# A GNN stack: the last of four column blocks is transposed on VectorE and sent through DRAM

## The chip, the cores and the metric

The kernel runs on one core of a Trainium2 chip. The metric is the device time in microseconds (us). Three runs of the kernel before took 2336.9, 2339.27 and 2341.34 us; the median, 2339.27 us, is the time before. Engines are called PE (TensorE, the matmuls), DVE (VectorE), ACT (ScalarE), POOL (GpSimd) and SP (SyncE, which issues DMAs).

## The reference, cut to what matters

Four layers of a graph network act on `x` of 32 batches, 512 nodes and 64 features; each adds its result to `x`, after a layer norm and a ReLU. The change touches the last layer, two graph attention steps with shared adjacency `graph` (512 x 512):

```python
def gat_layer(x, graph, W, b):
    h = x @ W
    s = jnp.einsum('bnd,bmd->bnm', h, h) * graph
    s = jnp.where(s == 0.0, NEG_INF, s)
    a = jax.nn.softmax(s, axis=2)
    return jnp.einsum('bnm,bmd->bnd', a, h) + b
heads = jax.vmap(lambda W, b: gat_layer(flow_x, graph, W, b))(Wh, bh)   # 8 heads of 128
x = jax.nn.leaky_relu(cat, negative_slope=0.01)                          # cat: the heads side by side
out = gat_layer(x, graph, W_out, b_out)                                  # 64 features
return jax.nn.leaky_relu(out, negative_slope=0.01)
```

So for each batch and head a matrix of 512 x 512 scores is made, exponentiated, and multiplied with the features. All arithmetic is float32.

## The kernel before, in words

**Stages.** Up to about 470 us of the profile the kernel runs layers 0 to 2. From there on it runs the last layer, and only that stage is changed (the features `hn`, `hs` of the first two batches are made a little earlier).

**Units.** The stage works on 144 units, each two attention problems at once (k = 0, 1): 128 units of class `Heads` (two heads of one batch, four units a batch) and 16 of class `Out` (the last step of two batches). The 512 nodes are C = 4 blocks of P = 128. A unit passes through these steps, with r a row block and j a column block of its score matrices:

- `scores(r)` (L386): matmuls into the PSUM tile `s_ps`, of which there are two buffers.
- `soft(r, mid)`: two reductions on DVE (L372) read `s_ps`, add the mask and give `s_att` and the row extremes `negmax`; two exponentials on ACT (L365) write row block r of `p_att` and the row sums. `mid` is called between, on DVE behind the reductions: it is `normalize` of an earlier unit.
- `transpose(j)` (L399): PE turns column block j of `p_att` in 16 transposes of 64 x 64 into two PSUM tiles `pt_ps` (tag "m", three buffers, shared with `y_ps`, `g_ps`, `gT_ps` and others). ACT copies the first (L405), at once; DVE copies the second (L407), at the end of the slot. Together they are `pt_att`.
- `values(j)` (L414): two matmuls with `pt_att` are added into `av`.
- `recips` (L424 to L434): DVE takes the reciprocals of the row sums and turns them in blocks of 32 x 32 (L426); SP writes them in four pieces to DRAM (`rec_row`), and reads them back in two, spread over the partitions (`recb`).
- `normalize` (L443): DVE multiplies `av` by `recb`. For `Heads`, `row_halves` then multiplies by the head's weights (`y_ps`, L526), ACT adds the bias (`cat`, L534) and DVE does the leaky ReLU (L311).

**Slots.** `planned` interleaves the units. In slot k, unit u does the step whose offset is off = k - 4u: scores at -1 to 2, soft at 0 to 3, transposes at TR = 5 to 8, values at VA = 6 to 9, normalize at END = 9, recips at 5. So a unit starts every four slots, each slot holds the steps of three or four units, and "slot 0 to 3 of a unit" below means the offset modulo 4. Inside a slot the order on each engine is that of the calls in `slot`, and it is kept as written for PE, DVE and ACT; DMAs on SP and POOL are placed by the framework. On PE it is scores, then `row_halves`, transposes, values, products for `Out` (`gT_ps`, L565); where `row_halves` has work (`led`), transposes come after the values. On DVE it is the two reductions, `normalize`, the copy of `pt_ps`, the leaky ReLU, recips, and `prep_late`.

**Features.** Once a batch, in slot 2, `prep_late` of `Heads` normalizes the features (`hn`, L474 and L475), takes their greatest values for a check of special cases at the end (`least`, L478), and POOL multiplies them by the root of the degrees, twice, into both halves of `hs` (L483). PE transposes `hs` in slot 3 (`hx_ps`, L290), ACT copies it (`hx`, L292), and `g_ps` (L508) is made of it in the next slot.

Of the kernel before, what the change touches and what calls it, by code (L numbers as in the profile page):

```python
# [8 lines left out]
F32 = mybir.dt.float32  # L9
# [5 lines left out]
P = 128  # L15
# [7 lines left out]
def fast_form(  # L23
# [29 lines left out]
    G = min(8, B)  # L53
    NG = B // G
    F2 = 2 * F

    const = ctx.enter_context(tc.tile_pool(name="const", bufs=1))
    xpool = ctx.enter_context(tc.tile_pool(name="xpool", bufs=1))
# [254 lines left out]
    class Pair:  # L313
# [4 lines left out]

        def begin(self):
            self.p = pbuf.tile([P, 2, C, N], F32, name="p_att")
            self.sum = tiny.tile([P, 2, C], F32, name="sum_att")
            self.negmax = tiny.tile([P, 2, C], F32, name="negmax")
            self.pts = {}
# [55 lines left out]
        def scores(self, r):  # L381
# [3 lines left out]
            for k in range(2):  # L385
# [2 lines left out]
                    start=True, stop=True,  # L388
                )

        def transpose(self, j):
            pt = pbuf.tile([P, 2, N], F32, name="pt_att", bufs=2)
            self.pts[j] = [pt[:, k] for k in range(2)]

            ps = [ps_m.tile([P, 2, C, F], F32, name="pt_ps", tag="m") for half in range(2)]
            for k in range(2):
                for r in range(C):
                    for half in range(2):
                        nc.tensor.transpose(  # L399
                            ps[half][:, k, r],  # L400
                            self.p[halves(half), k, r, j * P : (j + 1) * P],
                            ident[halves(half), halves(half)],
                        )
            pth = pt.rearrange("p k (r half q) -> p k r half q", r=C, half=2)
            nc.scalar.copy(pth[:, :, :, 0, :], ps[0])  # L405

            return lambda: nc.vector.tensor_copy(pth[:, :, :, 1, :], ps[1])  # L407

        def values(self, j):
            pt = self.pts.pop(j)  # L410
            if j == 0:
                self.av = ps_v.tile([P, N], F32, name="av")
            for k in range(2):
                nc.tensor.matmul(  # L414
                    self.av[halves(k), :], lhsT=self.v(k, j), rhs=pt[k],
                    start=(j == 0), stop=(j == C - 1),
                )

        def recips(self):

# [36 lines left out]
    class Heads(Pair):  # L457
# [11 lines left out]
        def prep_late(self, step):  # L469
            b = self.b  # L470
            if step == -2 and self.i == 0:
                mean, rstd = (t[:, b % 2, :, None].to_broadcast([P, C, F]) for t in flow_stats[b // 2])
                h = early.tile([P, C, F], F32, name="hn3", bufs=3)
                nc.vector.tensor_tensor(h, xs[b // G][:, b % G], mean, OP.subtract)  # L474
                nc.vector.scalar_tensor_tensor(  # L475
                    h, h, 0.0, rstd, op0=OP.max, op1=OP.mult
                )
                nc.vector.tensor_reduce(  # L478
                    least[:, b * C : (b + 1) * C], h, AX.X, OP.max
                )  # L480
                hs = early.tile([P, C, 2, F], F32, name="hs3", bufs=2)
                for k in range(2):
                    nc.gpsimd.tensor_tensor(  # L483
                        hs[:, :, k, :], h, root_d[:, :, None].to_broadcast([P, C, F]), OP.mult
                    )
                Heads.hs[b] = hs
                Heads.hn[b] = h

# [160 lines left out]
    def planned(units, products):  # L649
# [15 lines left out]
        def slot(k):  # L665
            for u, r in at(k, -1):
                u.scores(r)

            led = list(led_in(k))
            for u, off in led:
                u.row_halves(off)

            while exps:
                exps.pop(0)()

            copies = []

            def transposes():  # L680
                for u, j in at(k, TR):
                    copies.append(u.transpose(j))

            if not led:
                transposes()
            for u, j in at(k, VA):
                u.values(j)
            for u, j in at(k, VA - 1, 1):
                u.make_v()
            for n, u in products:  # L690
                u.product(k - n * C)
            for u, j in at(k, -3 * C, 3 * C):
                u.prep_pe(j - 2 * C)
            if led:
                transposes()
            for u, j in at(k, END, 5):
                u.end_pe(j)

            def mid():
                for u, j in at(k, END, 1):  # L700
                    u.normalize()

            now = list(at(k, 0))
            for u, r in now:
                exps.append(u.soft(r, mid))
            if not list(led_in(k + 1)):
                while exps:
                    exps.pop(0)()
            if not now:
                mid()  # L710
            for copy in copies:
                copy()
            for u, j in at(k, END, 5):
                u.end_late(j)
            for u, j in at(k, TR, 1):
                u.recips()
            for u, j in at(k, -3 * C, 3 * C):
                u.prep_late(j - 2 * C)

# [971 lines left out]
```

## Time and profile before

| | |
|---|---|
| median of three runs | 2339.27 us |
| the profiled execution, its time | 2340.76 us |
| its span | 2338.9 us |
| PE busy | 2248.0 us, 19066 instructions |
| DVE busy | 1794.3 us, 4366 instructions |
| ACT busy | 1576.3 us, 3674 instructions |
| POOL busy | 68.4 us, 104 instructions |
| transposes L399 | 9216, 415.6 us busy |
| copies of `pt_ps`: DVE L407, ACT L405 | 576 of 687 ns, 576 of 582 ns |
| HBM read, written | 43.98 MB, 4.78 MB |

Busy times say how long an engine had an instruction in work; spans of neighbouring instructions overlap, so the time from start to start is what one really costs in a row. The chain that ended last goes back from the last instruction, at each step to what released it; its shares say where the time of the run lay. A row of the timeline begins with the start and the length in us; "x4" means that four instructions are merged in it. In a table by windows each row has a stretch, its length, then busy time and count of PE, PEld, DVE, ACT and POOL, the granted clock, the busy share of the DMA engines, and GB/s. On SP and POOL a DMA's row is the time to issue it; the transfer follows.

### The profile page before, as it was taken

The page shows a single profiled execution, that of the slowest core. Times are in us where ns is not written, and L with a number is a line of the kernel's source. Part 1 is how long each engine was busy: PE and PEld are TensorE (multiplying, and loading weights), DVE is VectorE, ACT ScalarE, POOL GpSimd, SP SyncE. Part 2 cuts the span into 40 slices and gives each one's busy share as a digit, 9 for nine tenths or more (in the row PEclk, how much of TensorE's full clock was granted, in tenths as well). Part 3 has the DMA queues.
Part 4 walks back from the last instruction along what each step waited for, and adds up shares of the span by engine and source line. Part 5 has one row for each costly group of instructions (what it writes and reads, how often), then busy time and mean ns, then how long its engine had stood idle before and what let it go on. Part 6 is the DMA issues. An engine that isn't in the chain of part 4 may idle for free.

```text
span 2338.9 us, 49561 instructions
## 1 busy us (share of the span) xinstructions
PE 2248.0 (96%) x19066; PEld 1086.8 (46%) x19066; DVE 1794.3 (77%) x4366; ACT 1576.3 (67%) x3674; POOL 68.4 (3%) x104
## 2 busy tenths in 40 slices
PE   7999998799999999999999999999999999999997
PEld 4676776644444444444444444444444444444443
DVE  6788878677878787878787878787878787878776
ACT  3444433287777777777777777677777777877775
POOL 2000000000000000000000000000000000000000
PEclk9999999599999999999999999999999999999999
DMA  4000000000001000000000000000000000000001
GB/s 125 1 1 1 2 1 1 1 24 20 29 20 29 20 29 19 29 20 29 20 28 20 29 20 29 19 29 20 29 20 28 20 29 20 24 20 24 24 20 39
DMA packets 44645, 53.11 MB, mean 23 GB/s; under 512 B 15928, under 2 KB 25312, under 8 KB 44272
## 3 DMA queue, kind: packets, MB, share of 16 engines
q1 hardware_dynamic: 43888, 49.65, 6.9%
q8 instruction: 152, 2.49, 0.5%
q14 instruction: 93, 0.76, 0.1%
q0 software_dynamic: 512, 0.20, 0.1%
HBM read 43.98 MB, written 4.78 MB: 21 GB/s over the span
## 4 chain that ended last, share of the span: by engine, by line
PE 72%; DVE 4%; POOL 2%; issue 1%; ACT 0%; DMA 0%; SPq 0%; POOLq 0%; DVEq 0%
PE s_ps L386 23%; PE av L414 23%; PE pt_ps L399 13%; PE y_ps L526 5%; PE gT_ps L565 5%; PE g_ps L508 2%; DVE pt_att L407 2%; POOL hs L483 2%; PE hx_ps L290 1%; DVE hn L475 1%; DVE s_att L372 1%; DVE hn L474 0%; DVE gs L583 0%; PE gV_ps L576 0%; PE back_ps L449 0%
## 5 line engine op out<-in xcount | busy, mean ns | idle before, releaser
L365 ACT ACTIVATE p_att<-s_att,negmax 128x512 f32<-128x512 f32 x1152 | 827.7, 723 | 0.0
L372 DVE CUSTOM_DVE_ANT_0 s_att<-s_ps,flow_neg 128x512 f32<-128x512 f32 x1152 | 739.5, 679 | 2.4 <-PE s_ps L386 2.1
L407 DVE COPY pt_att<-pt_ps 128x512 f32<-128x512 f32 x576 | 395.5, 687 | 281.2 <-PE pt_ps L399 226.6
L386 PE MATMUL s_ps<-hx,g 64*128 64x512 f32 x2048 | 570.0, 634 | 5.7 <-DVE negmax L372 5.1
L414 PE MATMUL av<-pt_att,hn 128*64 128x512 f32 x2048 | 552.3, 618 | 0.0
L399 PEld LDWEIGHTS pt_ps<-ident,p_att 64*128 64x128 f32 x9216 | 373.6, 138 | 375.0 <-issue 228.0
L405 ACT COPY pt_att<-pt_ps 128x512 f32<-128x512 f32 x576 | 335.3, 582 | 157.9 <-PE pt_ps L399 152.2
L399 PE MATMUL pt_ps<-ident,p_att 64*128 64x64 f32 x9216 | 415.6, 226 | 2.8 <-DVE pt_att L407 0.9
L534 ACT ACTIVATE cat<-y_ps,bh 128x512 f32<-128x512 f32 x256 | 162.2, 684 | 168.4 <-PE y_ps L526 168.4
L386 PEld LDWEIGHTS s_ps<-hx,g 64*128 64x128 f32 x2048 | 156.1, 187 | 243.6 <-DVE negmax L372 180.6
L365 ACT ACTIVATION_READ_ACCUMULATOR p_att<-s_att,negmax 128x1 f32 x1152 | 224.6, 195 | 0.0
L443 DVE TENSOR_TENSOR o_att<-av,recb 128x512 f32<-128x512 f32 x144 | 99.6, 692 | 140.5 <-PE av L414 139.1
L414 PEld LDWEIGHTS av<-pt_att,hn 128*64 128x64 f32 x2048 | 101.2, 134 | 156.8 <-PE s_ps L386 87.2
L311 DVE SCALAR_TENSOR_TENSOR cat<-cat 128x1024 f32<-128x1024 f32 x128 | 155.5, 1215 | 0.0
L924 PE MATMUL acc<-v,s 64*128 64x65 f32 x2048 | 132.5, 291 | 1.5 <-DVE rec L935 0.8
L924 PEld LDWEIGHTS acc<-v,s 64*128 64x128 f32 x2048 | 129.5, 206 | 6.9 <-issue 2.6
L565 PE MATMUL gT_ps<-cat,wo_sb 128*64 128x512 f32 x512 | 131.7, 593 | 0.0
L526 PE MATMUL y_ps<-o_att,wh_sb 64*128 64x512 f32 x512 | 131.6, 591 | 0.0
L520 ACT COPY g<-g_ps 128x512 f32<-128x512 f32 x128 | 68.8, 589 | 84.2 <-PE g_ps L508 84.2
L833 PE MATMUL nt_ps<-adj_t,hn 128*128 128x512 f32 x256 | 116.2, 597 | 0.8 <-DVE hn L797 0.8
L386 PE MATMUL s_ps<-gs 64*128 64x512 f32 x256 | 72.4, 642 | 24.2 <-DVE gs L583 24.2
L372 DVE DVE_READ_ACCUMULATOR2_ANT negmax<- 128x1 f32 x1152 | 95.3, 83 | 0.0
(166 smaller groups left out, 1571.7 us busy)
## 6 DMA issues: line engine op xcount, KB each, us to landing
recb<-rec_row SPq DMA_DIRECT2D x288, 128.0 KB
rec_row<-rect SPq DMA_DIRECT2D x576, 1.0 KB
out_dram<-y SPq DMA_DIRECT2D x32, 128.0 KB
x<-in_x_dram SPq DMA_DIRECT2D x3, 1024.0 KB
x<-in_x_dram SPq DMA_DIRECT2D x4, 256.0 KB
adj_raw<-in_adj_dram SPq DMA_DIRECT2D x1, 1024.0 KB
mask<-mask SPq DMA_DIRECT2D x4, 256.0 KB
wh_sb<-in_L_gnn_Wh_dram SPq DMA_DIRECT2D x2, 256.0 KB
```

What stands on the lines that cost most here:

```text
L311: nc.vector.scalar_tensor_tensor(t, t, 0.01, t, op0=OP.mult, op1=OP.max)
L365: nc.scalar.activation(self.p[:, k, r, :], ns[:, k], AF.Exp, bias=self.negmax[:, k, r : r + 1], scale=-1.0, accum_out=self.sum[:, k, r : r ...
L372: nc.vector.tensor_tensor_reduce(out=ns[:, k], in0=ps[:, k], in1=flow_neg[:, r], scale=-1.0, scalar=BIG, op0=OP.add, op1=OP.min, accum_out ...
L386: nc.tensor.matmul(ps[:, k], lhsT=g[halves(k), r * P : (r + 1) * P], rhs=x[halves(k), :], start=True, stop=True,)
L399: nc.tensor.transpose(ps[half][:, k, r], self.p[halves(half), k, r, j * P : (j + 1) * P], ident[halves(half), halves(half)],)
L405: nc.scalar.copy(pth[:, :, :, 0, :], ps[0])
L407: return lambda: nc.vector.tensor_copy(pth[:, :, :, 1, :], ps[1])
L414: nc.tensor.matmul(self.av[halves(k), :], lhsT=self.v(k, j), rhs=pt[k], start=(j == 0), stop=(j == C - 1),)
L526: nc.tensor.matmul(ps, lhsT=wh_sb[halves(k), h, :], rhs=self.o[halves(k), :], start=True, stop=True,)
L534: nc.scalar.activation(self.cat[:, k], pss[k], AF.Identity, bias=bh[:, h : h + 1], scale=1.0)
L565: nc.tensor.matmul(self.gps[halves(k), :], lhsT=wo_sb[:, h, :], rhs=Heads.cat[b + k, h], start=(h == 0), stop=(h == H - 1),)
L924: nc.tensor.matmul(self.acc[k][:, r], lhsT=self.s[b // 2][halves(k), b % 2, r * P : (r + 1) * P], rhs=self.v[halves(k), b], start=(b == 0) ...
```

## The change

1. Column block j = 3 is no longer transposed on PE. `transposes` runs for j = 0 to 2. A new step `turn(r)`, at offsets 2 to 5 and on DVE behind `normalize`, turns row block r of that column block in squares of 32 x 32, from `p_att` into the SBUF tile `turn` (128 x 256 elements each). After r = 1 and r = 3, POOL issues a write of two row blocks to DRAM (`turn_row`, 256 KB in pieces of 512 bytes).
2. `route`, called with `recips`, reads the squares back in transposed order into `turned`: four reads of 128 KB, 32 partitions each, in pieces of 1 KB; two are issued by POOL and two by SP. `values(3)` takes `turned` in two halves of 256 columns, in steps of 32 elements.
3. The second PSUM copy of j = 0 and j = 2 goes from DVE to ACT, right behind the first; that of j = 1 stays on DVE.
4. `hs` is made by one DVE operation of 128 x 512 ahead of the `least` reduction, in place of two POOL operations of 128 x 256 behind it.

In the changed program's order SP has, for each unit, the four `rec_row` writes, the first read of `turned`, the two reads of `recb`, and the second read of `turned`; POOL has two `turn_row` writes and then two reads of `turned`.

```diff
+        def turn(self, r):
+            if r == 0:
+                self.turns = wk.tile([P, Q, C // 2, 2, 2, 32], F32, name="turn")
+                self.rows = dram.tile([P, Q, C // 2, P], F32, name="turn_row")
+            nc.vector.transpose(
+                self.turns[:, :, r // 2, :, r % 2].rearrange("p a k i -> p k a i"),
+                self.p[:, :, r, N - P :].rearrange("p k (a i) -> p k a i", i=32),
+            )
+            if r % 2:
+                nc.gpsimd.dma_start(
+                    self.rows[:, :, r // 2],
+                    self.turns[:, :, r // 2].rearrange("p a k r i -> p a (k r i)"),
+                )
+
+        def route(self):
+            rows = self.rows.rearrange("(b i) a g x -> a i b (g x)", b=Q)
+            pt = wk.tile([P, Q, C // 2, 2, 2, 32], F32, name="turned")
+            for a in range(Q):
+                (nc.sync if a % 2 else nc.gpsimd).dma_start(
+                    pt[a * 32 : (a + 1) * 32].rearrange("p b g k r i -> p b (g k r i)"), rows[a]
+                )
+            self.pts[C - 1] = [
+                pt[:, :, :, k].rearrange("p b g r i -> p g r b i") for k in range(2)
+            ]
...
             nc.scalar.copy(pth[:, :, :, 0, :], ps[0])
+            if j != 1:
+                nc.scalar.copy(pth[:, :, :, 1, :], ps[1])
+                return None
...
             for k in range(2):
-                nc.tensor.matmul(
-                    self.av[halves(k), :], lhsT=self.v(k, j), rhs=pt[k],
-                    start=(j == 0), stop=(j == C - 1),
-                )
+                parts = 2 if j == C - 1 and len(pt[k].shape) > 2 else 1
+                for g in range(parts):
+                    n = N // parts
+                    nc.tensor.matmul(
+                        self.av[halves(k), g * n : (g + 1) * n], lhsT=self.v(k, j),
+                        rhs=pt[k][:, g] if parts > 1 else pt[k],
+                        start=(j == 0), stop=(j == C - 1 and g == parts - 1),
+                    )
...
+                hs = early.tile([P, C, 2, F], F32, name="hs3", bufs=2)
+                nc.vector.tensor_tensor(
+                    hs, h[:, :, None].to_broadcast([P, C, 2, F]),
+                    root_d[:, :, None, None].to_broadcast([P, C, 2, F]), OP.mult,
+                )
                 nc.vector.tensor_reduce(
                     least[:, b * C : (b + 1) * C], h, AX.X, OP.max
                 )
-                hs = early.tile([P, C, 2, F], F32, name="hs3", bufs=2)
-                for k in range(2):
-                    nc.gpsimd.tensor_tensor(
-                        hs[:, :, k, :], h, root_d[:, :, None].to_broadcast([P, C, F]), OP.mult
-                    )
...
-                for u, j in at(k, TR):
+                for u, j in at(k, TR, C - 1):
                     copies.append(u.transpose(j))
...
             if not now:
                 mid()
+            for u, r in at(k, 2):
+                u.turn(r)
             for copy in copies:
-                copy()
+                if copy:
+                    copy()
             for u, j in at(k, END, 5):
                 u.end_late(j)
             for u, j in at(k, TR, 1):
                 u.recips()
+                u.route()
```

Here Q = P // 32 = 4.

More of the change, by code (lines that the diff above doesn't have):

```diff
@@ L55, in fast_form @@
     F2 = 2 * F
+    Q = P // 32
     const = ctx.enter_context(tc.tile_pool(name="const", bufs=1))
```

## The prediction

> **What bounds the kernel now.** I read the busy times first, then the chain that ended last, then the timeline of one ordinary stretch, then the waits at the places that the diff touches. The long second stage (from about 470 us) is the one concerned.
>
> ```profile
> PE 2248.0 (96%) x19066; PEld 1086.8 (46%) x19066; DVE 1794.3 (77%) x4366; ACT 1576.3 (67%) x3674; POOL 68.4 (3%) x104
> PE 72%; DVE 4%; POOL 2%; issue 1%; ACT 0%; DMA 0%; SPq 0%; POOLq 0%; DVEq 0%
> PE s_ps L386 23%; PE av L414 23%; PE pt_ps L399 13%; PE y_ps L526 5%; PE gT_ps L565 5%; PE g_ps L508 2%; DVE pt_att L407 2%; POOL hs L483 2%; PE hx_ps L290 1%; DVE hn L475 1%; DVE s_att L372 1%; DVE hn L474 0%; DVE gs L583 0%; PE gV_ps L576 0%; PE back_ps L449 0%
> ...
> 600.00:1000.00 400.00, 390.75 (x3312) 168.84 (x3312) 309.11 (x784) 301.91 (x723) 8.30 (x14) 1.00 0.08 25
> ```
>
> The last row is 400 us of that stage: PE busy 390.75 of 400, DVE 309, ACT 302. PE is nearly solid and carries 72% of the chain; transposes (L399) alone are 13% of it. One slot on PE without extras:
>
> ```profile
> 1224.92 1.13 PE L386 MATMUL s_ps<-hx,g 64*128 64x512 f32 x4
> 1225.88 0.66 PE L399 MATMUL pt_ps<-ident,p_att 64*128 64x64 f32 x16
> 1226.47 1.08 PE L414 MATMUL av<-pt_att,hn 128*64 128x512 f32 x4
> 1227.48 1.13 PE L386 MATMUL s_ps<-hx,g 64*128 64x512 f32 x4
> ...
> 1226.70 0.69 DVE L372 CUSTOM_DVE_ANT_0 s_att<-s_ps,flow_neg 128x512 f32<-128x512 f32 x1
> 1227.32 0.69 DVE L407 COPY pt_att<-pt_ps 128x512 f32<-128x512 f32 x1
> ```
>
> Scores, 16 transposes, values, next scores: 2.56 us from start to start. In the chain these three are 1.06, 0.49 and 1.01 us. The scores at 1227.48 overwrite the s_ps that the reduction starting at 1226.70 frees at about 1227.32 (the copy's start), so DVE is only 0.16 us ahead of PE here. Unit periods, from the starts of the reciprocals (L424), repeat over nine units: 11.3, 13.3, 11.3, 14.9, 14.7, 13.7, 13.3, 11.9, 12.2 us, 116.5 in all.
>
> The place of the features:
>
> ```profile
> 1235.34 0.42 DVE L478 TENSOR_REDUCE least<-hn 128x4 f32<-128x256 f32 x1
> 1235.48 1.19 POOL L483 TENSOR_TENSOR hs<-hn,root_d 128x256 f32<-128x256 f32 x2 [47.43 <-DVE hn L475]
> 1235.20 1.08 PE L414 MATMUL av<-pt_att,hn 128*64 128x512 f32 x4
> 1236.72 0.66 PE L290 MATMUL hx_ps<-ident,hs 128*128 128x128 f32 x4 [0.44 <-POOL hs L483]
> 1237.31 1.13 PE L386 MATMUL s_ps<-hx,g 64*128 64x512 f32 x4
> ```
>
> PE ends its values at 1236.21 and waits 0.5 us for POOL's product, 32 times in the run.
>
> The two round trips through DRAM at the very end, and what a GpSimd transfer shows in the opening:
>
> ```profile
> 2323.52 1.16 DMA rec_row<-rect
> 2325.49 3.22 DMA recb<-rec_row
> ...
> 1224.00:1224.50 0.50, 0.50 (x4) 0.10 (x4) 0.50 (x3) 0.50 (x2) 0.00 (x0) 1.00 0.37 135
> 4.46 1.54 POOL L93 DMA_DIRECT2D wl<-in_L_gnn_net_params_dram  x3
> wg<-in_L_gnn_W_dram POOLq DMA_DIRECT2D x2, 16.0 KB, 4.8
> ```
>
> A small write lands 1.16 us after its issue; the second 128 KB read 3.22 us after. In an ordinary unit the reads issued from 1222.86 move data from about 1224.0 to 1225.9 (the DMA share, last but one figure of the row, is zero before), so 1.15 us pass before the first byte, and 1 us or so after the last.
>
> [...] The trace has only a 128x32 one, 0.21 us (L426), beside 0.19 for a 128x8 reciprocal[...]. [...] the trace has only the opening's 4.6 to 8.0 us beside bulk loads. [...] here recb waits for rec_row 278 times, 129.7 us.
>
> **The change part by part.** Column block 3's transposes go from PE: 144 units x 16, 0.49 us a group on the chain (0.65 only where the following scores shrink to 0.91, so the pair costs the same): 144 x 0.49 = -70.6 us, if PE stays the bound.
>
> Values of block 3 become four matmuls of 256 columns for two of 512. [...] The shape in steps of 32 columns isn't in the trace; 0.15 us at most, which is what this line already takes above the same-shaped gT_ps (1.01 against 0.86 us). I take 0.05: +7 us, ends +2 and +22.
>
> PSUM copies: DVE loses three of four (0.60 us from start to start), ACT gains two and loses one. ACT has per unit 8 exponentials at 0.71, five copies at 0.48, and cat: under 10 us of 11, and its copies come before the slot's exponentials, sooner than DVE's did. Cost 0, hidden by ACT's 100 us of slack in 400.
>
> DVE turns: four a unit, each 128x256. The nearest row, a 128x256 operation at L474, is 0.41 long; independent operations here follow 0.08 us before the end, so 0.37 apart. Bounds: 0.3, and 0.6 if it costs like a 128x512 copy. DVE per unit: -3 x 0.60 + 4 x 0.37 = -0.3 us. But where they stand counts. Slot 3 and 0 of a unit hold: two reductions 1.22, turn(1) 0.37, leaky 1.17, two reductions 1.22. Counted from the copy's end at 1223.14 this frees s_ps at 1227.12; PE, without block 3's transposes, asks at 1226.99. Stall 0.13 us in the three ordinary units of nine: 48 x 0.13 = +6 us. Where slot 0 also holds g_ps or gT_ps (0.86 us), PE arrives later and nothing is lost. turn(0) stands in the 0.8 us for which DVE waited for transposes anyway, turn(2) and turn(3) behind reductions.
>
> Features on DVE: one 128x512 product, 0.61 between starts, in place of two on POOL (1.19). They are ready at about 1236.0, so PE's 0.5 us wait goes. Nobody waits for least before the end. But it and both reductions of slot 3 now follow 0.61 later: these end at 1237.6, and the scores that began at 1237.31 wait for s_ps until 1237.65. g_ps then covers the rest; by slot 1 PE is 0.22 us ahead of before, not 0.49. So 32 x 0.27 = +8.6 us; ends -17 (the wait gone, no new one) and +15.
>
> The trip through DRAM. turn(3) stands behind normalize on DVE (0.61), itself behind the previous unit's last values; it ends 0.98 us after normalize starts. The values that need it start 1.1 us before the next normalize. So a unit can't be shorter than L + 2.1 us, L being the trip. Step by step: handoff to POOL 0.17 (1235.31 to 1235.48); its descriptors 1.0 (64 rows took 0.51; 512 rows aren't in the trace: 0.5 to 2.5); then 1.16 as for rec_row and 1.2 for 256 KB in 512-byte rows (the final outputs moved 256 KB in about 1 us). The write has landed at 3.5. On SP's queue the changed program stands so: four rec_row, the first turned read, two recb, the second turned read. All behind the first turned read wait for the write: four issues of 0.48, data of four transfers in a row on one queue from 1.15 to about 3.8, 1.0 to land: 4.8. POOL's two reads (0.6 us each to issue) are in before. L = 8.3, between 7 and 10.5: floor 10.4. The shortest unit would be 10.9, so nothing is lost. Queued behind them on SP stand only the next rec_row and, after an Out unit, the y writes, some 8 us later. turn(0) also waits for the writes of two units before, long landed. recb, held 2 us longer, lands by 8 us, and normalize needs it 1 us after the turned block: free, and late with it if L grows. In the drain the last unit (9.7 us) shows the floor: +2 us.
>
> Sum: -70.6 + 7 + 6 + 8.6 + 2 = -47 us. On the profiled execution (2340.76 us, 2338.9 of it span; the median, 2339.27, is 1.5 below): 2292 for the median.
>
> **The rivals.** (1) The trip is late; this one ends slower. Shortened units are 10.9, 12.9, 10.9, 14.4, 14.2, 13.2, 12.9, 11.4, 11.7, sixteen cycles of them. A floor of 12.0 costs 2.2 + 0.6 + 0.3 = 3.1 a cycle, 50 us: the gain is gone at L = 9.9. At L = 10.5 it is 5.5 x 16 = 88 us, 2380. For it: [...] an unmeasured size, two hops, and 4.6 us as the shortest GpSimd landing, of which two make 9.2. Against: that opening moved 232 to 376 GB/s, this stage 25. At L = 9.5 the loss is 26 us: 2318. (2) DVE becomes the bound: a turn of 0.69. Then 0.32 more in 48 + 32 places, +25 us: 2317. For: slack of 0.16[...]. (3) All of PE's time is won and the wait for features too: -70.6 - 17 = 2252. For: DVE falls by 0.3 a unit; against: the two places worked out above.
>
> **How the numbers follow.** Forecast 45%, own range 2275 to 2308; (3) 12%; (2) or a trip slightly late, 2308 to 2334, 16%; within 0.2% (4.7 us, about what a measurement can tell) 4%; (1) 23%. Faster 0.73, same 0.04, slower 0.23. The range, 2260 to 2368, leaves out about 5% below, and above it a trip over 10.3 us, 14%.
>
> **What would show it.** Right: L399 at 6912, its chain share near 10%; PE still over 95% in the stage; the values of block 3 hardly waiting for DMA; periods near 10.9 in the short units; scores after hx waiting for negmax. Wrong: PE waiting for turned in the short units, all nine periods levelled at one floor; POOL issues of over 2 us; turns of 0.6 us; or values on turned over 1.1 us.

## The result, and the profile after

The changed kernel takes 2350.9 us (median of five runs, 2348.07 to 2362.17) against 2339.06 us for the kernel before (five runs, 2336.09 to 2341.34). The ratio is 1.0059, with a 95% interval of 1.0033 to 1.0086: slower by 11.8 us, where 47 us less was forecast. The profiled execution's span is 2348.9 us, 10.0 more than before.

First the page of the changed kernel: busy times, and the chain that ended last, by engine and by line.

```profile
PE 2176.4 (93%) x17338; PEld 1037.8 (44%) x17338; DVE 1741.1 (74%) x4542; ACT 1635.4 (70%) x3818; POOL 400.2 (17%) x616
PE 49%; DMA 13%; DVE 8%; issue 7%; SPq 3%; POOL 1%; ACT 1%; DVEq 0%; POOLq 0%; ACTq 0%
PE av L449 16%; PE s_ps L389 16%; DMA turned<-turn_row 10%; PE pt_ps L427 6%; PE gT_ps L601 5%; PE y_ps L562 4%; SPq L470 3%; DVE s_att L375 3%; DMA turn_row<-turn 3%; DVE pt_att L438 2%; PE g_ps L544 2%; DVE hs L515 1%; DVE hn L511 1%; POOL turn_row L403 1%; DVE hn L510 0%
```

PE lost 71.6 us of work, but it also fell from 96% busy to 93%. The chain tells more: PE carries 49% of it where it carried 72%, and DMA, which had none, now carries 13%, of which the reads of `turned` are 10%. SPq, time in which SP was issuing, is new too, with 3% on L470, the reads of `recb`. The stretch of 400 us answers to the one shown of before:

```profile
600.00:1000.00 400.00, 376.34 (x2927) 159.49 (x2924) 296.82 (x819) 313.40 (x753) 79.67 (x124) 1.00 0.39 106
```

PE is busy for 376 us, not 391: 24 us of 400 idle, in a stage that left 9 idle before. What PE waited for, from the list of waits of the changed kernel (engine, line, releaser; us in total, times, longest):

```profile
PE av L449 <- DMA turned<-turn_row: 70.4, 64, 4.8
DVE o_att L479 <- PE av L449: 335.4, 144, 7.0
PE s_ps L389 <- DVE negmax L375: 22.4, 34, 0.7
```

Values of column block 3 waited for `turned` 64 times, 70.4 us in all. DVE's idle time ahead of `normalize` grew to 335 us. The third row is the place of the features. The same two places in the kernel before, which has no `turned`:

```profile
DVE o_att L443 <- PE av L414: 139.1, 143, 2.5
PE s_ps L386 <- DVE negmax L372: 5.1, 14, 0.4
```

From the timeline of the changed kernel, first a short slot with the leaky ReLU, and then the place of the features:

```profile
1246.27 1.18 DVE L312 SCALAR_TENSOR_TENSOR cat<-cat 128x1024 f32<-128x1024 f32 x1
1246.54 1.13 PE L389 MATMUL s_ps<-hx,g 64*128 64x512 f32 x4
...
1247.60 1.08 PE L449 MATMUL av<-pt_att,hn 128*64 128x512 f32 x4
...
1247.99 0.69 DVE L375 CUSTOM_DVE_ANT_0 s_att<-s_ps,flow_neg 128x512 f32<-128x512 f32 x1
...
1248.74 1.13 PE L389 MATMUL s_ps<-hx,g 64*128 64x512 f32 x4
```

```profile
1232.56 0.69 DVE L515 TENSOR_TENSOR hs<-hn,root_d 128x512 f32<-128x512 f32 x1
...
1233.17 0.41 DVE L519 TENSOR_REDUCE least<-hn 128x4 f32<-128x256 f32 x1
1233.50 0.66 PE L291 MATMUL hx_ps<-ident,hs 128*128 128x128 f32 x4
...
1234.11 0.68 DVE L375 CUSTOM_DVE_ANT_0 s_att<-s_ps,flow_neg 128x512 f32<-128x512 f32 x1
...
1234.86 1.13 PE L389 MATMUL s_ps<-hx,g 64*128 64x512 f32 x4 [0.71 <-DVE negmax L375]
```

Scores, values and next scores take 2.20 us from 1246.54 to 1248.74. Scores take 1.06 and values 1.01 in the chain, so 0.13 us is a stall: the last reduction starts only at 1247.99, behind the leaky ReLU. At the second place PE no longer waits for the features (`hx_ps` has no releaser), but the scores behind it wait 0.71 us for the reductions.

One trip through DRAM that came late, from the timeline of the changed kernel:

```profile
1240.49 0.69 DVE L479 TENSOR_TENSOR o_att<-av,recb 128x512 f32<-128x512 f32 x1 [1.44 <-PE av L449]
1241.10 0.43 DVE L398 STREAM_TRANSPOSE turn<-p_att 128x256 f32<-128x256 f32 x1
...
1241.83 0.71 POOL L403 DMA_DIRECT2D turn_row<-turn  x1 [5.65 <-DVE rec L460]
1241.89 1.29 SPq L465 DMA_DIRECT2D rec_row<-rect  x4
...
1244.64 0.32 SPq L412 DMA_DIRECT2D turned<-turn_row  x1
...
1245.13 1.42 SPq L470 DMA_DIRECT2D recb<-rec_row  x2
1245.15 1.14 POOL L412 DMA_DIRECT2D turned<-turn_row  x2 [2.61 <-PE s_ps L389]
...
1246.60 0.59 SPq L412 DMA_DIRECT2D turned<-turn_row  x1
1246.64 0.72 POOL L403 DMA_DIRECT2D turn_row<-turn  x1 [0.36 <-DVE turn L398]
...
1250.79 1.09 PE L449 MATMUL av<-turned,hn 128*64 128x256 f32 x8 [0.44 <-DMA turned<-turn_row]
```

turn(3) ends at 1241.53, POOL issues the write at 1241.83, and SP's first read, which waits for that write, starts at 1244.64, so by 3.11 us the write has landed. SP then issues two reads of `recb`, and only at 1246.60 the last read of `turned`. The values start at 1250.79, 9.26 us after the turn. The chain of the same stretch shows what released them:

```profile
1245.13 0.78 SPq L470
1245.96 0.59 SPq L470
1246.60 3.95 DMA turned<-turn_row
1250.79 1.09 PE av L449 x8
```

It runs through SP's two issues of `recb` into the last read of `turned`, which takes 3.95 us to land. And how much the DMA engines moved meanwhile, from a table by windows of the changed kernel:

```profile
1245.30:1246.40 1.10, 1.10 (x13) 0.36 (x9) 1.10 (x6) 1.10 (x5) 0.98 (x2) 1.00 0.52 118
1246.40:1248.00 1.60, 1.60 (x8) 0.50 (x8) 1.60 (x4) 1.60 (x5) 0.72 (x1) 1.00 0.69 204
1248.00:1250.40 2.40, 2.30 (x24) 0.96 (x20) 2.24 (x9) 2.04 (x7) 0.00 (x0) 1.00 0.92 247
1250.40:1252.00 1.60, 1.21 (x10) 0.78 (x12) 0.08 (x1) 1.60 (x4) 0.00 (x0) 1.00 0.00 0
```

After 1248.0 the engines are 92% busy at 247 GB/s until the block has landed, then at rest. From 1245.3 to then they moved some 1050 KB (118 GB/s for 1.1 us, 204 for 1.6, 247 for 2.4). The unit's four reads of `turned` (512 KB), its two of `recb` (256 KB) and a `turn_row` write of the next unit (256 KB, issued at 1246.64) make 1024.

Over the 63 units of the steady part whose values waited, the medians from the end of turn(3) are: write issued 0.30, SP's first read begins 3.12 (landed, as SP sees it), POOL's reads begin 3.62, the issue of SP's last read done 5.74, values 10.06 us.

Where the 10.0 us of the spans lie: -4.3 ahead of the first unit's reciprocals (472.2 us before, 467.9 after), which the change hardly touches; +6.6 from there to the last unit's (1849.8 and 1856.4); +7.7 from there to the end (16.9 and 24.6).

### The profile page after: what moved, and what is told of

It reads as the page before. It is cut to its first block, busy times and chain, and to the rows that moved or that the text cites. A ratio compares the mean times of both kernels' runs of the same rounds, so it can differ in the third digit from the quotient of the medians.

```text
span 2348.9 us, 47698 instructions
## 1 busy us (share of the span) xinstructions
PE 2176.4 (93%) x17338; PEld 1037.8 (44%) x17338; DVE 1741.1 (74%) x4542; ACT 1635.4 (70%) x3818; POOL 400.2 (17%) x616
## 4 chain that ended last, share of the span: by engine, by line
PE 49%; DMA 13%; DVE 8%; issue 7%; SPq 3%; POOL 1%; ACT 1%; DVEq 0%; POOLq 0%; ACTq 0%
PE av L449 16%; PE s_ps L389 16%; DMA turned<-turn_row 10%; PE pt_ps L427 6%; PE gT_ps L601 5%; PE y_ps L562 4%; SPq L470 3%; DVE s_att L375 3%; DMA turn_row<-turn 3%; DVE pt_att L438 2%; PE g_ps L544 2%; DVE hs L515 1%; DVE hn L511 1%; POOL turn_row L403 1%; DVE hn L510 0%
## 5 line engine op out<-in xcount | busy, mean ns | idle before, releaser
L389 PE MATMUL s_ps<-hx,g 64*128 64x512 f32 x2048 | 574.5, 638 | 26.9 <-DVE negmax L375 22.4
L403 POOL DMA_DIRECT2D turn_row<-turn x288 | 207.2, 719 | 1234.6 <-DVE rec L460 891.0
L449 PE MATMUL av<-pt_att,hn 128*64 128x512 f32 x1536 | 414.3, 618 | 0.0
L427 PEld LDWEIGHTS pt_ps<-ident,p_att 64*128 64x128 f32 x6912 | 279.5, 139 | 279.1 <-issue 185.1
L433 ACT COPY pt_att<-pt_ps 128x512 f32<-128x512 f32 x432 | 251.2, 581 | 114.6 <-PE pt_ps L427 113.2
L427 PE MATMUL pt_ps<-ident,p_att 64*128 64x64 f32 x6912 | 310.8, 226 | 1.3 <-ACT pt_att L433 0.6
L398 DVE STREAM_TRANSPOSE turn<-p_att 128x256 f32<-128x256 f32 x576 | 252.7, 439 | 0.8 <-ACT p_att L368 0.8
L412 POOL DMA_DIRECT2D turned<-turn_row x288 | 163.2, 573 | 409.4 <-PE pt_ps L427 177.2
L438 DVE COPY pt_att<-pt_ps 128x512 f32<-128x512 f32 x144 | 99.1, 688 | 150.7 <-PE pt_ps L427 150.7
L449 PE MATMUL av<-turned,hn 128*64 128x256 f32 x1024 | 141.4, 394 | 54.3 <-DMA turned<-turn_row 54.1
L435 ACT COPY pt_att<-pt_ps 128x512 f32<-128x512 f32 x288 | 171.5, 596 | 0.0
L449 PEld LDWEIGHTS av<-pt_att,hn 128*64 128x64 f32 x1536 | 75.9, 134 | 193.7 <-issue 92.5
```

The lines of the kernel that those rows point to most:

```text
L389: nc.tensor.matmul(ps[:, k], lhsT=g[halves(k), r * P : (r + 1) * P], rhs=x[halves(k), :], start=True, stop=True,)
L398: nc.vector.transpose(self.turns[:, :, r // 2, :, r % 2].rearrange("p a k i -> p k a i"), self.p[:, :, r, N - P :].rearrange("p k (a i) -> ...
L403: nc.gpsimd.dma_start(self.rows[:, :, r // 2], self.turns[:, :, r // 2].rearrange("p a k r i -> p a (k r i)"),)
L412: (nc.sync if a % 2 else nc.gpsimd).dma_start(pt[a * 32 : (a + 1) * 32].rearrange("p b g k r i -> p b (g k r i)"), rows[a])
L427: nc.tensor.transpose(ps[half][:, k, r], self.p[halves(half), k, r, j * P : (j + 1) * P], ident[halves(half), halves(half)],)
L435: nc.scalar.copy(pth[:, :, :, 1, :], ps[1])
```

## The experiments

The question was first whether the trip is the whole loss, then which part of the trip, and last whether the sizes of the other steps held. One of them, the third, did not reach what it was made for. Ratios are to the kernel before on the same chip; its medians there were 2341.4 us (experiments 1 to 4), 2341.47 (5 to 8), 2341.59 (9 and 10) and 2339.79 (11).

**1. Values of block 3 don't wait.** All turns, writes and reads remain, but values(3) multiplies a constant tile; column block 3's part of the result is left out. `turned` has one buffer, which makes room for the tile.

```diff
             self.pts[C - 1] = [
-                pt[:, :, :, k].rearrange("p b g r i -> p g r b i") for k in range(2)
+                still[:, :, :, k].rearrange("p b g r i -> p g r b i") for k in range(2)
             ]
```

> The values of block 3 read a constant tile of ones in place of turned, so the part of the result that comes from column block 3 is left out; every turn, write and read still runs. Theory (the wait for the trip is the whole loss): the forecast without the trip, 2338.9 - 71 + 6 + 9 = about 2284 us, so 0.97 to 0.98 of before. Rival (the added traffic or the added DVE and ACT work slows the engines themselves): close to the 2351 of the change, over 2330.

Measured: 2277.09 us (2276.93 to 2281.18), ratio 0.9727 (0.9702 to 0.9752). The same 400 us:

```profile
600.00:1000.00 400.00, 389.72 (x3052) 164.05 (x3052) 309.44 (x854) 327.19 (x786) 82.96 (x129) 1.00 0.40 110
```

PE is back at 389.72 us busy, although the DMA share is 0.40, as in the changed kernel (0.39). The theory that the traffic itself slows the engines fell; waiting for it costs the difference of the two spans, 2348.9 - 2275.1 = 73.8 us. Of this, 70.3 us lie between the first and the last unit's reciprocals (1856.4 against 1786.1 us).

**2. The turn ahead of normalize.** DVE turns in `mid`, before `normalize` of the earlier unit; nothing is left out.

```diff
             def mid():
+                for u, r in at(k, 2):
+                    u.turn(r)
                 for u, j in at(k, END, 1):
                     u.normalize()
...
-            for u, r in at(k, 2):
-                u.turn(r)
```

> The change with the turns put ahead of normalize on DVE. Theory (the trip starts late because turn(3) stands behind normalize, which waits for the previous unit's values): turn(3) starts about 1.9 us and ends 2.5 us sooner in the short units, so a trip of 10 us is nearly hidden: 2285 to 2310 us. Rival (the trip is bound by the DMA engines' rate, so that starting sooner only queues sooner): over 2335 us.

Measured: 2272.8 us (2271.24 to 2276.16), ratio 0.9704 (0.9678 to 0.973): 3% faster than the kernel before. Values waited for `turned` once, 1.9 us, in the drain. From this kernel's timeline:

```profile
1234.54 0.45 DVE L398 STREAM_TRANSPOSE turn<-p_att 128x256 f32<-128x256 f32 x1 [0.93 <-ACT p_att L368]
1235.28 0.71 POOL L403 DMA_DIRECT2D turn_row<-turn  x1 [4.55 <-DVE turn L398]
1236.04 1.09 PE L449 MATMUL av<-turned,hn 128*64 128x256 f32 x8
1237.19 0.69 DVE L479 TENSOR_TENSOR o_att<-av,recb 128x512 f32<-128x512 f32 x1 [2.21 <-PE av L449]
```

turn(3) runs at 1234.54, as soon as its exponentials are done. In the changed kernel it stood behind `normalize`, and so behind the previous unit's values; here these start at 1236.04 and normalize at 1237.19, 2.65 us after the turn. The trip no longer starts where the previous trip ended. The kernel is even 4 us below experiment 1, where no values waited: in the profiled runs one unit in nine takes 11.21 instead of 11.39 us, and the end after the last reciprocals 19.8 instead of 21.7. But the order that the framework gave SP changed with it: one or both reads of `turned`, `rec_row`, the other read of `turned` where one is left, and only then `recb`. So two things changed here; experiment 11 separates them.

**3. The first write behind turn(2).** The `turn_row` write of the next unit fell into the reads (1246.64 above). Here its call stands one slot later, behind turn(2); nothing is left out.

```diff
-            if r % 2:
+            if r >= 2:
                 nc.gpsimd.dma_start(
-                    self.rows[:, :, r // 2],
-                    self.turns[:, :, r // 2].rearrange("p a k r i -> p a (k r i)"),
+                    self.rows[:, :, r - 2],
+                    self.turns[:, :, r - 2].rearrange("p a k r i -> p a (k r i)"),
                 )
```

> The change with the first turn_row write issued after turn(2), one slot later, so that it does not fall among the previous unit's reads. Theory (the reads take 7 us from the write's landing, not 4.8, because the next unit's write of 256 KB and the recb reads share the DMA engines with them): the trip shrinks from 10.1 by 1 us or more, 2300 to 2330 us. Rival (the 7 us are issue and landing latency): no change, 2345 to 2357 us.

Measured: 2347.54 us (20 runs, 2341.22 to 2355.04), ratio 1.0022 (1.0012 to 1.0033). Values waited 63 times, 67.2 us, and started 10.04 us after the turn: as in the changed kernel. But the edit did not move the write. From this kernel's timeline:

```profile
1246.11 0.44 DVE L398 STREAM_TRANSPOSE turn<-p_att 128x256 f32<-128x256 f32 x1
...
1246.85 0.72 POOL L403 DMA_DIRECT2D turn_row<-turn  x1 [0.37 <-DVE turn L398]
...
1248.80 0.44 DVE L398 STREAM_TRANSPOSE turn<-p_att 128x256 f32<-128x256 f32 x1
```

The write needs the data of turn(0) and turn(1) alone, and POOL still issues it 0.29 us after turn(1), 2.4 us before turn(2) ends (medians, the same in the changed kernel). So this run tests nothing of the theory that the next unit's write collides with the reads. The DMA packets in the changed kernel's trace do better, since there the write comes early for some units and late for others. Take the units in which SP had issued its last read 5.3 us after the turn: in 18 the next write was issued before 5.3 us, in 28 after 6.8 us, and the last data on SP's queue came at 9.02 and 8.85 us (medians). By this comparison the write costs the reads some 0.2 us.

This kernel does what the changed kernel does, yet it lies 6.1 us above the kernel before, and the changed kernel 11.8. Differences of that size between two experiments are safer read from the periods of units than from whole times.

**4. Features back on POOL.** Two POOL operations behind the `least` reduction; the rest as changed, nothing left out.

```diff
-                hs = early.tile([P, C, 2, F], F32, name="hs3", bufs=2)
-                nc.vector.tensor_tensor(
-                    hs, h[:, :, None].to_broadcast([P, C, 2, F]),
-                    root_d[:, :, None, None].to_broadcast([P, C, 2, F]), OP.mult,
-                )
                 nc.vector.tensor_reduce(
                     least[:, b * C : (b + 1) * C], h, AX.X, OP.max
                 )
+                hs = early.tile([P, C, 2, F], F32, name="hs3", bufs=2)
+                for k in range(2):
+                    nc.gpsimd.tensor_tensor(
+                        hs[:, :, k, :], h, root_d[:, :, None].to_broadcast([P, C, F]), OP.mult
+                    )
```

> The change with the features' product back on POOL behind least. Theory (on DVE it costs 0.27 us net at 32 places, since the score reductions come later): 5 to 12 us faster than the change, 2340 to 2346. Rival (it was right to leave POOL, which now issues DMAs and where PE waits 0.5 us): 5 to 17 us slower, 2356 to 2368.

Measured: 2362.48 us (2359.02 to 2366.41), ratio 1.0092 (1.0066 to 1.0118): 21.1 us above the kernel before on its chip, where the changed kernel was 11.8 above: about 9 us slower than the changed kernel. PE's wait for the features is the largest after that for `turned`; the row is from this kernel's waits, the others are from its timeline:

```profile
PE hx_ps L291 <- POOL hs L519: 37.9, 32, 4.2
```

```profile
1239.09 0.42 DVE L511 SCALAR_TENSOR_TENSOR hn<-hn,rstd 128x256 f32<-128x256 f32 x1
...
1239.64 1.13 POOL L412 DMA_DIRECT2D turned<-turn_row  x2 [3.15 <-PE pt_ps L427]
1240.79 1.19 POOL L519 TENSOR_TENSOR hs<-hn,root_d 128x256 f32<-128x256 f32 x2
1242.03 0.66 PE L291 MATMUL hx_ps<-ident,hs 128*128 128x128 f32 x4 [1.47 <-POOL hs L519]
```

The product starts 0.02 us after POOL has issued its two reads of `turned`. From the end of `hn` to POOL's start it was 0.17 us in the kernel before; here it is 0.7 to 1.6 in 28 of 32 batches, and there always within 0.02 us after such an issue. With PE 0.49 us earlier and POOL 0.55 later the wait doubled, and a unit with features takes 13.27 us, as before the change (13.28), not 13.04. That is 0.23 x 32 = 7 us of the 9.

**5. Features on DVE alone.** The kernel before with only that edit; the diff is the reverse of the one in 4.

> The kernel before with the features' product moved to DVE, ahead of least, and nothing else. By the prediction's step (PE's wait of 0.5 us goes, the scores that follow wait for s_ps 0.34 us later than before): 32 x 0.34 = 11 us slower, 2350. Rival (POOL's product was a plain loss of 0.5 us each): 10 to 17 us faster, 2325 to 2331.

Measured: 2349.63 us (20 runs, 2348.72 to 2357.67), ratio 1.0031 (1.0021 to 1.0042). A unit with features takes 13.62 us instead of 13.28, which makes 0.34 x 32 = 11 us; the medians differ by 8.2. `least` and both reductions follow later, and PE's short wait for POOL turns into one for `negmax`.

**6. The reads of `recb` last.** On SP each unit's order is four `rec_row`, two `turned`, two `recb`, and turn(3) stays behind normalize. Nothing is left out.

```diff
             for q in range(P // 32):
                 nc.sync.dma_start(
                     row[:, q * 32 : (q + 1) * 32], rect[q * 32 : q * 32 + 2 * C, :]
                 )
+            self.row = row
+
+        def spread(self):
+            row = self.row
             self.recb = wk.tile([P, N], F32, name="recb")
...
                 u.recips()
                 u.route()
+                u.spread()
```

> The change with SP's order for each unit made four rec_row, two reads of turned, two reads of recb: nothing is left out, and turn(3) still stands behind normalize. Theory (the last read of turned is late because two recb reads, issue and data, stand in front of it on SP's queue): it is issued 1.1 to 1.9 us sooner, the trip falls from 10.1 to about 8.5 us, under what the short units bear: 2275 to 2300 us. Rival (what the DMA engines must move in the trip sets its length, in whatever order): 2335 to 2351 us.

Measured: 2289.38 us (2288.46 to 2293.83), ratio 0.9772 (0.9743 to 0.9801). Four waits for `turned` remain, 6.3 us in all. It is 12 us above experiment 1 (4 of it, in the profiled runs, ahead of the stage), and a few units of 11.9 to 12.6 us still occur where 10.95 to 11.5 is possible: the trip is now only just short enough. A trip from this kernel's timeline:

```profile
1222.06 0.43 DVE L398 STREAM_TRANSPOSE turn<-p_att 128x256 f32<-128x256 f32 x1
1222.79 0.71 POOL L403 DMA_DIRECT2D turn_row<-turn  x1 [5.65 <-DVE rec L460]
...
1225.59 1.32 SPq L412 DMA_DIRECT2D turned<-turn_row  x2
1226.10 1.13 POOL L412 DMA_DIRECT2D turned<-turn_row  x2 [2.60 <-PE s_ps L389]
1227.09 1.09 SPq L474 DMA_DIRECT2D recb<-rec_row  x2
...
1231.25 1.09 PE L449 MATMUL av<-turned,hn 128*64 128x256 f32 x8
```

Both reads of `turned` are issued by 1226.91, the values start without a wait at 1231.25, 8.76 us after the turn, and this unit lasts 10.95 us, the shortest period of experiment 1. Over all units SP's last read of `turned` is issued 3.93 us after the turn (median), 1.7 sooner than in the changed kernel. From the pages of the two kernels, DMA issues (KB each, median us from issue to landing), first the changed kernel and then this one:

```profile
turned<-turn_row POOLq DMA_DIRECT2D x288, 128.0 KB, 4.1
```

```profile
turned<-turn_row POOLq DMA_DIRECT2D x288, 128.0 KB, 3.5
```

POOL's reads land sooner as well, by 0.6 us, though their own queue is unchanged; that fits data of `recb` in their way. POOL's second read is now the last to come: all four waits that remain end 0.09 us after it has landed, where in the changed kernel the values waited 0.2 to 2.8 us longer, for SP's last read.

**7. No reads of `recb`.** Normalize multiplies by a constant tile instead; the row sums' part of the result is left out.

```diff
-            self.recb = wk.tile([P, N], F32, name="recb")
-            for k in range(2):
-                nc.sync.dma_start(
-                    self.recb[halves(k), :],
-                    row[k * C : (k + 1) * C]
-                    .rearrange("(o r) p -> o (r p)", o=1)
-                    .to_broadcast([F, N]),
-                )
+            self.recb = even
```

> The change without the recb reads: normalize multiplies by a constant, so the softmax's division is left out of the result; rec_row is still written. Theory (recb's place and its 256 KB make the trip long): trip of 8 us or less, 2270 to 2290 us. Rival (write and reads of the turned block alone take 10 us): 2340 to 2351 us.

Measured: 2280.17 us (2277.56 to 2282.57), ratio 0.9732 (0.9705 to 0.976). Two waits, 4.8 us, both in the last two units; POOL's reads land in 3.0 us. In these two units the values start 8.34 and 7.71 us after the turn, where the changed kernel's take 10.00 and 10.38. So the `recb` reads cost 1.7 and 2.7 us, 2.2 on average; and here too both waits end 0.09 us after POOL's second read has landed.

**8. PSUM copies alone.** The kernel before, with the second copy of column blocks 0 and 2 on ACT; block 3's stays on DVE. Nothing is left out.

```diff
             nc.scalar.copy(pth[:, :, :, 0, :], ps[0])
+            if j % 2 == 0:
+                nc.scalar.copy(pth[:, :, :, 1, :], ps[1])
+                return lambda: None
```

> The kernel before with the second PSUM copy of column blocks 0 and 2 moved to ACT, and nothing else. By the prediction's step (hidden by ACT's slack): within 5 us of before, 2334 to 2344. Rival (ACT's later exponentials hold up the transposes): 5 us slower or more.

Measured: 2334.24 us (20 runs, 2331.0 to 2342.42), ratio 0.9972 (0.9963 to 0.998). One unit in nine, that of 12.18 us, falls to 11.72; 0.45 x 16 = 7 us.

**9. Turn first, and `least` two slots later.** Experiment 2 with the reduction to `least` away from the place of the features; nothing left out.

```diff
-                nc.vector.tensor_reduce(
-                    least[:, b * C : (b + 1) * C], h, AX.X, OP.max
-                )
                 Heads.hs[b] = hs
                 Heads.hn[b] = h
+            if step == 0 and self.i == 0:
+                nc.vector.tensor_reduce(
+                    least[:, b * C : (b + 1) * C], Heads.hn[b], AX.X, OP.max
+                )
```

> The turns ahead of normalize, and the reduction to least (0.41 us, used only at the end) moved two slots later; nothing left out. If the 0.7-us waits of the 32 scores behind hx (22.4 us in all) come from the features and least standing together ahead of that slot's two score reductions, taking 0.34 us from between start and start brings the reductions forward by as much at 32 places: about 2272 - 11 = 2262, hx units at 12.7 instead of 13.0, and the negmax waits near 0.35 us. If the reduction merely stalls the slot that it moves to, or PE is bound there by something else, 2269 to 2276 and hx units at 13.0.

Measured: 2264.61 us (2261.95 to 2266.26), ratio 0.966 (0.9635 to 0.9686). From the waits of this kernel:

```profile
PE s_ps L389 <- DVE negmax L375: 12.4, 33, 0.5
```

12.4 us where 22.4 stood, and units with features take 12.71 us instead of 13.03: 0.32 x 32 = 10 us; the lead over the kernel before grew from 68.6 us in experiment 2 to 77.0. It is the fastest of all, with its equal in the next.

**10. The same, with `recb` last on SP.** Experiments 9 and 6 together; nothing left out.

> As the run before, and SP's queue in the order rec_row, turned, turned, recb, recb; nothing left out. If the trip was already short enough once the turn stood ahead of normalize, this adds nothing: within 4 us of the run before, and no wait for turned. If the last turned read behind recb still held up some units, up to 5 us less. If recb, now last, comes late for normalize, longer units and slower than the run before by over 5 us.

Measured: 2264.5 us (2262.38 to 2265.8), ratio 0.9662 (0.9636 to 0.9687): no different from 9. It tells nothing more: in the trace of 9 `recb` already stands behind the reads of `turned`, so the edit moved nothing on SP.

**11. Turn first, SP in the order of the changed kernel.** Experiment 2 with SP's order written out: four `rec_row`, a read of `turned`, two of `recb`, the second of `turned`. Nothing is left out.

```diff
             for a in range(Q):
+                if a == Q - 1:
+                    self.spread()
                 (nc.sync if a % 2 else nc.gpsimd).dma_start(
...
             mybir.EngineType.Activation,
+            mybir.EngineType.SP,
         }
```

`spread` holds the reads of `recb`, as in experiment 6; `SP` stands in the list of engines whose order is kept as written.

> The turns ahead of normalize, with SP held to the order of the changed kernel: rec_row, turned, two recb, turned; nothing left out. Experiment 2 had changed both the place of the turn and, through it, SP's order. If the earlier start of the trip is enough by itself, values still hardly wait and the time is that of experiment 2, 2268 to 2278, though the last turned read is issued over 5 us after the turn and the trip lasts some 10 us. If it was the order on SP that helped there, values wait some 60 times as in the changed kernel, and it is above 2320. In between, part of each.

Measured: 2279.1 us (2277.76 to 2282.48), ratio 0.9744 (0.9728 to 0.976). From the waits of this kernel:

```profile
PE av L451 <- DMA turned<-turn_row: 8.3, 6, 3.2
```

Six waits are left of 64, and the periods are those of experiment 2 (10.95, 11.21 and 11.52 us for the short units), although SP issues its last read 6.47 us after the turn (median). So the earlier start of the trip is enough by itself. The better order adds the difference of the leads, 68.6 - 60.7 = 8 us, of which these waits, two of them in the last two units, are 6.4 (8.3 against 1.9).

## Why the prediction was wrong

The forecast was 2292 us, and the rival that ends slower came true, near its own break-even point.

**The step that failed** is in the trip: "four issues of 0.48, data of four transfers in a row on one queue from 1.15 to about 3.8, 1.0 to land: 4.8". The order on SP had been read rightly, with two `recb` reads ahead of the last read of `turned`. But what they cost was too small in each part. From the landed write the four issues are done after 2.6 us (5.74 - 3.12), not 1.9, and from there to the values it is 4.3 us (10.06 - 5.74), not 2.9: together 6.9. The sum left out what else moves at that time: POOL's two reads, taken to be in before, begin 0.5 us after SP's first, and the next unit's write joins them, 512 KB in the same 4 us, at engines up to 92% busy.

What was missing, 10.06 - 8.3 = 1.8 us, is only in part the price of the `recb` reads. Experiment 7 puts it at 2.2 us, but the sum had charged some 1.3 for them already (two of the four transfers, 0.66 us each): 0.9 too little. The rest stands in the trip without them, where the same sum gives 7.0 us and 8.0 was measured, and where POOL's second read, not SP's, comes last. That its data are slow because the other transfers share the engines fits, but no run shows it apart; the next unit's write is a small part, by the comparison in experiment 3. Either of two edits removes the loss, and that is shown. Experiment 6 takes the `recb` reads from ahead and nearly all of the waits go. Experiments 2 and 11 move the start of the trip: the floor of L + 2.1 exists only because turn(3) stands behind normalize, and there it doesn't (in 11 with the last read issued even later than in the changed kernel). In experiment 6 the last read of `turned` is issued 1.7 us sooner once `recb` stands behind it, 3.93 us after the turn (median).

"recb, held 2 us longer, … free" belongs to the same error. It was asked only what the delay does to `recb`, not what `recb` does to the read behind it.

**The floor and its price.** With 10.06 us in place of 8.3 the floor of a unit is 12.16. The periods as predicted then lose 1.26 twice, 0.76 and 0.46 us in a cycle of nine, 3.74 x 16 = 60 us, and -47 + 60 gives 2352 us, where 2350.9 was measured. So the break-even of 9.9 us was near the truth. That the sum fits so well is partly luck: the wait cost 74 us, not 60, since the short units don't level at one floor but scatter, nearly all from 11.4 to 13.0 us, and the drain is longer, and the gain that it ate was larger too (below). In the steady part the two cancel: nine units in a row take 116.6 us on average, where the kernel before takes 116.5.

**First half of the trip:** landed at 3.11 us, predicted 3.5. POOL's issue of 512 rows took 0.72 us, not 1.0, far from the bound of 2.5. Right within its bounds.

**Transposes and shortened periods.** Experiment 1 shows the change without its wait. Its nine units sum to 112.4 us, 4.1 less than before; the step-by-step sum gives 49 / 16 = 3.1 less. So the wait hid a gain of about 64 us, where 47 was reckoned. The parts, from the periods:

- Ordinary short units went from 11.29 to 10.95: -0.34, where -0.49 for the transposes and +0.13 for the stall give -0.36. The stall in the slot shown is 0.13. Right.
- The split of values costs nothing: eight matmuls on `turned` take 1.02 us from start to start, against 1.01. Predicted +7 us, of which the 0.05 us a unit was an estimate; the result is near its lower end.
- Turns: 0.44 us long, 0.37 from start to start. Right; the rival in which DVE becomes the bound fell. So did the one in which all of PE's time is won, 2252 us: without the wait it was 2277.
- The copies were put at 0 and gave more. Experiment 8: 7 us from one unit in nine. In experiment 1 that unit falls from 12.18 to 11.39, 0.3 more than the transposes explain. A unit with `Out` work falls from 14.91 to 14.20, 0.2 more, which wasn't traced.

**Features.** The size was right: scores behind `hx_ps` wait 0.7 us for `negmax` 32 times, PE's wait for POOL is gone, and a unit with features gains 0.24 us where -0.49 + 0.27 gives 0.22. But the sign of the step was wrong for this kernel. It was charged with 8.6 us against the old place, and the same edit alone costs 8 us (experiment 5); in the changed kernel it saves 7 to 9 (experiment 4, by periods and by whole times), since the product would stand on POOL behind the issues of the new reads. What else is on an engine's queue after the change was asked of SP, not of POOL.

**The drain** was put at +2 us. From the last reciprocals to the end it takes 24.6 us instead of 16.9, +7.7: the last unit's values wait 4.81 us for `turned`. In experiment 1, where they don't, it still takes 21.7, because normalize waits for `recb` there, behind the first read of `turned`.

Of the signs of error that the prediction named, PE waiting for `turned` in the short units was there to see. Long POOL issues, turns of 0.6 us and slow values were not.

## What to carry to other kernels

When a value goes by a DMA trip, price the last read of it by all that stands ahead on its queue and all that moves beside it in the same microseconds: here two reads of `recb` ahead of it held back its issue by 1.7 us, and POOL's reads, on another queue, landed in 4.1 us with `recb` ahead on SP and in 3.5 with it last there (the changed kernel and experiment 6). Put transfers that nobody needs yet behind it. Look also at where the trip starts: here one call moved ahead of another on DVE broke a loop from one unit's values to the next unit's turn, and turned a loss of 0.6% into a gain of 3%. And when an engine gets new DMAs to issue, ask what compute is left on it: the same edit was a loss of 8 us alone and a gain of 7 to 9 beside them.

## What was not expected of the hardware

- POOL's issue of a write in 512 pieces of 512 bytes takes 0.72 us, and one of a read in pieces of 1 KB 0.57; the opening's three loads take 1.54.
- A read of 128 KB that POOL issued landed in 2.9 to 4.1 us (medians of four kernels): 4.1 in the changed kernel, 3.5 with `recb` later, 3.0 without `recb`, and 2.9 in experiment 2.
- SP and POOL wait for the same write, and in the changed kernel POOL starts 0.5 us later (3.62 against 3.12 us after the turn, medians).
- Without waits, in experiment 1, the DMA share of 0.40 and 110 GB/s in the stage cost PE little that could be seen: 389.7 of 400 us busy, against 390.75 before with a share of 0.08 and 25 GB/s.
- The unchanged stage ahead varies from run to run: the first unit's reciprocals come at 467.3 us in experiment 1, at 467.9 in the changed kernel, at 472.2 in the kernel before, and at 477.7 in experiment 8. Periods of units told more here than whole times: in the steady part of the kernel before, 105 of 108 repeat to 0.02 us (the others are 15.28 and 15.27 where 14.91 is usual, and 13.57 where 13.28 is).
